# A graph network layer on one core: a new table of places that orders every step on its engine

## The chip, the cores and the metric

The kernel runs on one core of a Trainium2 chip. The core's engines work side by side: TensorE (PE in the profile, its weight loads PEld), VectorE (DVE), ScalarE (ACT), GpSimd (POOL) and the queue that issues most DMA transfers (SP). Each engine takes its instructions in the order in which the program gives them, and instructions of different engines wait for each other by semaphores. The metric is device time in microseconds (us); the median of three runs is given.

## The reference

A message passing layer on 128 graphs of 64 nodes with 128 features each. `x` is 128×64×128, `adj` is 128×64×64, zeros and ones; a node has itself as a neighbour, and some one in eight of the pairs is an edge.

```python
def _layernorm(x, g, b):
    mu = mean(x, -1); var = mean(square(x - mu), -1)
    return (x - mu) * rsqrt(var + 1e-5) * g + b
def _mlp(x, w0, b0, g0, be0, w1, b1, g1, be1, w2, b2):
    h = _layernorm(relu(x @ w0 + b0), g0, be0)
    h = _layernorm(relu(h @ w1 + b1), g1, be1)
    return h @ w2 + b2
pair_feats = concatenate([f_i, f_j], -1)          # every pair (i, j) of nodes of a graph
messages = _mlp(pair_feats, msg_...) * coupling_matrix[..., None]     # adj
agg = sum(messages, axis=2)
updated = part_feats + _mlp(concatenate([part_feats, agg], -1), upd_...)
```

All in float32.

## The kernel before

Only the edges are worked on. Two graphs make a pair p (64 of them); each graph gets 640 slots for its edges, and the slots of all graphs are cut into 160 chunks n of 512 edges. Five chunks make a quad q (32 of them), four pairs and ten chunks a block b (16 of them).

For a pair, `distance` (ACT, d), `make_tp` (DVE, tp) and `node_rows` (POOL) turn the adjacency into numbers of the first node of each edge slot; `marks` (PE, into the bank mk) and `compare` (DVE, j) find the second node; `stack` (DMA) puts both into one array s, which holds a one for each node of each edge. For a block, `turn_x` transposes x, and `rows` multiplies it by the two halves of the first weight (PE, into mu), from which `rows_hi` (ACT, abh) and `rows_lo` (DVE, abl) make a coarse and a fine part.

For a chunk: `gather` multiplies abl and abh by s (PE, into hps), `relu0` (ACT, h), `turn_h` (PE transposes into hT), `stats0` (DVE, two instructions st). The first layer norm is folded in: `root_of` (ACT, m20_sd) gives a standard deviation per edge, with which the bias of the second layer is scaled, either by `seed` (ACT, four instructions into the bank z0 or z1, for half of the chunks) or by `seed_all` (POOL, u). `layer1` (PE) then multiplies h by the weight w1c into that bank, `relu1` (ACT, or DVE with u) makes y, `stats1` (DVE) its statistics. For a quad, `var1_step` (POOL), `root1_of` (ACT), `inverse_of` (DVE) and `weights` (POOL, w) give each edge's factor, and `reduce` (PE, ys) sums y by node, once per block. A block's update follows in steps on four pairs: `sums_out` (ACT, ysum), `turn` (PE, ma) and `turn_out` (ACT, ysumT, uhT, uyT), the three layers (PE), their outputs and statistics (DVE), and the DMA of the result.

Every accumulator of PE (hps, hT, mk, ys, ma, mu, z0, z1) has one bank, so a step that fills a bank again waits for the engine that empties it.

The start has steps of its own (`marks_here`, `compare_here`, `rows_here` for the first two pairs) and matmuls without use that keep PE going (`keep_busy`, into ys).

No step is issued where it stands in the code. Each is entered into a plan with a nominal chunk n and a tag, and a table WHEN adds a number to its place:

```python
def at(n, tag, fn, *args):
    v = args[0] if args else 0
    v = v.b if isinstance(v, Unit) else v
    t = WHEN.get(f"{fn.__name__}{tag}", {}).get(n % 10 if 14 <= n < 138 else 100 + v, 0)
    plan.append((SCALE * n + t, len(plan), fn, args))
...
for _, _, fn, args in sorted(plan, key=lambda v: v[:2]):
    fn(*args)
```

SCALE is 144, so one chunk is 144 units. For n from 14 to 137 the table has one entry for each n modulo 10, so the order repeats every block; before and after, each step has an entry of its own (key 100 + its index). The sorted plan is the order of emission, and so the order on every engine. A second path for graphs with more edges than fit stands behind a condition and is not run with these inputs.

Of the kernel before, what the change touches and what calls it, by code (L numbers as in the profile page):

```python
# [9 lines left out]
F32 = mybir.dt.float32  # L10
# [42 lines left out]
    "count_out.0": {100: 79},
    "degrees": {9: -369, 101: -144, 102: -4, 115: -419},
    "degrees.0": {100: 58},
    "distance": {0: -532, 3: 185, 5: -470, 8: -359, 103: 34, 104: 302, 105: -163, 106: 312,
        107: -610, 108: 189, 158: -893, 159: -639, 160: -591, 161: -589, 162: 13, 163: -1137},
    "distance.0": {100: 163},
    "distance.1": {101: 208},
    "distance.2": {102: 283},  # L60
    "empties.0": {100: 156},
    "empties.1": {100: 154},
    "empties.10": {100: -158},
    "empties.11": {100: 84},
# [1592 lines left out]
```

## Time and profile before

| | |
|---|---|
| median of 3 runs (lowest to highest) | 496.4 us (495.78 to 496.48) |
| span of the profiled execution | 495.0 us |
| what lies around the span, by the median | 1.4 us |
| PE busy | 484.8 us (98%), 5947 instructions |
| DVE busy | 462.3 us (93%), 1225 |
| ACT busy | 397.9 us (80%), 907 |
| POOL busy | 353.0 us (71%), 563 |
| mean granted clock of TensorE | 0.995 |

The profiled execution has no time of its own beside its span, so the median of the runs stands for it. The span runs from the first to the last instruction. A row of the page's groups gives the line, engine, operation, output and inputs, the number of instructions, their busy time and mean length in ns, then the idle time of that engine just before them and what ended most of it. A row of the timeline gives the start, the length, the engine, the line, the operation, how many like it are joined, and in brackets the idle time before and its releaser. Matmuls overlap in a pipeline, so their rows are longer than the time from one to the next.

### The profile page before, as it was taken

Reading aid. Unit: us, or ns where it says so; the run is one execution under the profiler, and the core shown is the slowest. Engines: PE = TensorE matmul, PEld = TensorE weight load, DVE = VectorE, ACT = ScalarE, POOL = GpSimd, SP = SyncE. Lnnn points to the kernel's source line nnn. Section 1 sums busy time; section 2 is a strip of 40 time slices with the busy share of each in tenths; the row PEclk is TensorE's granted clock in tenths of the full one; section 3 lists DMA queues with packets and bytes.
Section 4 is the critical chain, followed back from the end, with each engine's and each line's share of the span. In section 5 each row is a group of like instructions: output and inputs, shape, how many; then the busy total and the mean of one; then the engine's idle time right before and its main releaser. Section 6 shows DMA issues by size and latency. Waiting matters only on the chain.

```text
span 495.0 us, 15915 instructions
## 1 busy us (share of the span) xinstructions
PE 484.8 (98%) x5947; PEld 461.3 (93%) x5947; DVE 462.3 (93%) x1225; ACT 397.9 (80%) x907; POOL 353.0 (71%) x563
## 2 busy tenths in 40 slices
PE   7999999999999999999999999999999999999994
PEld 5798999999999999999999999999999999999994
DVE  7989989999999999999999999999999999989975
ACT  7999978888787887878878787887878778767753
POOL 3276768878778787777779777787877678576661
PEclk9999999999999999999999999999999999999998
DMA  4676685667656575765757657466956775564311
GB/s 123 140 176 150 135 142 120 129 139 152 143 121 140 117 155 130 154 137 114 147 109 164 130 134 158 110 139 130 170 126 115 161 102 132 134 102 107 61 39 47
DMA packets 91474, 63.55 MB, mean 128 GB/s; under 512 B 57473, under 2 KB 75522, under 8 KB 91394
## 3 DMA queue, kind: packets, MB, share of 16 engines
q1 hardware_dynamic: 91106, 62.36, 60.4%
q8 instruction: 49, 0.80, 0.7%
q14 instruction: 31, 0.25, 0.1%
q10 hardware_dynamic: 288, 0.13, 0.1%
HBM read 7.15 MB, written 4.19 MB: 23 GB/s over the span
## 4 chain that ended last, share of the span: by engine, by line


## 5 line engine op out<-in xcount | busy, mean ns | idle before, releaser
L984 PE MATMUL z<-w1c,h 128*128 128x128 f32 x1280 | 190.0, 275 | 0.0
L984 PEld LDWEIGHTS z<-w1c,h 128*128 128x128 f32 x1280 | 171.7, 191 | 3.9 <-issue 0.4
L936 ACT ACTIVATE h<-hps,b0c 128x512 f32<-128x512 f32 x160 | 109.0, 681 | 42.3 <-PE hps L931 40.7
L627 DVE BATCH_NORM_STATS2 st<-hT 128x6 f32<-128x256 f32 x320 | 122.2, 418 | 15.3 <-PE hT L941 12.7
L627 DVE BATCH_NORM_STATS2 st<-y 128x6 f32<-128x256 f32 x320 | 125.3, 419 | 0.0
L978 ACT ACTIVATE z<-b1b,m_sd 128x128 f32<-128x128 f32 x320 | 118.4, 371 | 6.5
L941 PE MATMUL hT<-ident,h 128*128 128x128 f32 x640 | 113.3, 276 | 0.2 <-DVE st L627 0.2
L931 PE MATMUL hps<-s,abl 128*128 128x512 f32 (+3 forms) x256 | 97.0, 381 | 0.6 <-DVE abl L865 0.3
L971 POOL TENSOR_TENSOR u<-b1b,m_sd 128x512 f32<-128x512 f32 x80 | 87.5, 1103 | 7.8 <-ACT m_sd L635 7.7
L931 PE MATMUL hps<-s,abh 128*128 128x512 f32 (+3 forms) x256 | 92.2, 365 | 0.0
L941 PEld LDWEIGHTS hT<-ident,h 128*128 128x128 f32 x640 | 77.2, 141 | 2.9 <-PE z L984 0.6
L1027 POOL TENSOR_TENSOR w<-oh,m_q 128x192 f32<-128x192 f16 x126 | 65.2, 533 | 17.2 <-DVE m_q L656 9.6
L914 DVE TENSOR_TENSOR j<-mk,cmpt 128x320 fp32r<-128x320 f32 x124 | 59.3, 478 | 2.8 <-PE mk L906 1.2
L995 ACT ACTIVATE y<-z 128x512 f32<-128x512 f32 x80 | 47.9, 598 | 17.3 <-PE z L984 17.0
L611 DVE CUSTOM_DVE_ANT_0 y<-z,u 128x512 f32<-128x512 f32 x80 | 54.2, 678 | 1.7 <-PE z L984 0.2
L931 PEld LDWEIGHTS hps<-s,abl 128*128 128x128 f32 x256 | 48.8, 191 | 5.2 <-ACT ab L851 2.0
L889 POOL CAST i<-tp 128x640 fp32r<-128x640 f16 x58 | 41.8, 721 | 16.6 <-DMA s<-i 11.5
L874 ACT ACTIVATE d<-slot,mid 128x640 f16<-128x640 f16 x64 | 52.4, 822 | 0.4 <-DVE tp L880 0.3
L931 PEld LDWEIGHTS hps<-s,abh 128*128 128x128 f32 x256 | 49.5, 193 | 0.2
L645 POOL TENSOR_TENSOR m_v<-m_v,st 128x20 f32<-128x20 f32 x31 | 7.2, 232 | 57.5 <-DVE st L627 54.6
L1042 PE MATMUL ys<-y,w 128*32 128x128 f32 x1488 | 44.1, 274 | 0.0
L1042 PEld LDWEIGHTS ys<-y,w 128*32 128x32 f32 x1488 | 39.6, 110 | 2.6 <-issue 1.7
(193 smaller groups left out, 883.2 us busy)
## 6 DMA issues: line engine op xcount, KB each, us to landing
s<-j SPq DMA_DIRECT2D x124, 160.0 KB, 2.8
...
oh<-tp SPq DMA_TRANSPOSE x64, 3.5
...
```

Source lines behind the costliest of these rows:

```text
L611: nc.vector._custom_dve(TENSOR_ADD_SAT, out=o, in0=ps, in1=sb, s0=BIG, s1=0.0)
L627: nc.vector.bn_stats(st, src.rearrange("p t c -> p c t"))
L874: nc.scalar.activation(D[p], slot, AF.Abs, bias=blocks[b]["mid"][:, q:q + 1], scale=-1.0)
L914: nc.vector.tensor_tensor(JR[p][:, c], MK.pop((p, k))[:, 0:HC], cmpt[:, c], op=ALU.is_equal)
L931: nc.tensor.matmul(HP[n][:, c:c + w], lhsT=blocks[g // (2 * PB)]["ab", g // 4 % 2][k][:, g % 4, :], rhs=S[g // 2][:, g % 2, e:e + w], star ...
L936: nc.scalar.activation(H[n], HP.pop(n), AF.Relu, bias=b0c)
L941: nc.tensor.transpose(HT[n][:, t, :], H[n][:, t * P:(t + 1) * P], ident)
L971: nc.gpsimd.tensor_tensor(U[n], bc(W["b1b"], CH), SR[q][:, k:k + CH].unsqueeze(2).to_broadcast([P, CH, C]), op=ALU.mult)
L978: nc.scalar.activation(z_of(n)[:, t, :], W["b1b"], AF.Copy, scale=SR[q][:, k:k + 1])
L984: nc.tensor.matmul(ps[:, t, :], lhsT=H[n][:, t * P:(t + 1) * P], rhs=W["w1c"], start=by_vector(n) and t == 0, stop=True, skip_group_check= ...
L1027: (nc.vector if p == NP - 2 else nc.gpsimd).tensor_tensor(WT[p][:, g], oh, qs, op=ALU.mult)
L1042: nc.tensor.matmul(YS[b][g * N + m * HN:g * N + (m + 1) * HN, k, :], lhsT=w[:, g, m, u, :], rhs=y, start=(u == 0), stop=(u == TH - 1), til ...
```

## The change

The table WHEN is replaced as a whole: every number in it is new, for the start, for the ten chunks that repeat, and for the end. The operations, their sizes and their engines are the same. So that a step's two halves may come in either order, the code no longer lets the second half drop what the first one made: an entry is kept, or made by whichever half comes first. Line numbers behind the table move on by 44 to 49.

```diff
 WHEN = {
-    "bias0": {3: -1230, 112: -1975, 113: -1986, 114: 89},
+    "bias0": {3: -273, 112: -1205, 113: 4627, 114: -250},
...
-            nc.gpsimd.tensor_tensor(pos, blk.pop("rk"),
+            nc.gpsimd.tensor_tensor(pos, blk["rk"],
...
-                ps = blk["x_ps"] = bank()
+                ps = blk["x_ps", q0] = bank()
...
-            if k0 == 0:
+            if ("ab", half) not in blk:
...
-            if t:
-                del HT[n]
...
-            if t0:
-                del H[n]
...
-            if q == 0:
-                u.st = updp.tile([P, PB // 2, 6], F32, name=o + "_st", bufs=2)[:, 0:u.n // 2, :]
+            if o not in u.sts:
+                u.sts[o] = updp.tile([P, PB // 2, 6], F32, name=o + "_st", bufs=2)[:, 0:u.n // 2, :]
+            u.st = u.sts[o]
...
-            if q0 == 0:
-                u.usdb = wide("usdb", u)
+            u.usdb = wide("usdb", u)
...
+        def stacked(p):
+            if p not in S:
+                S[p] = sp.tile([P, 2, CAP], F32R, name="s")
+            return S[p]
...
-            nc.scalar.copy(S[p][0:N, g, :], TP[p][g * N:(g + 1) * N])
+            nc.scalar.copy(stacked(p)[0:N, g, :], TP[p][g * N:(g + 1) * N])
```

The order that follows from the table is shown at three places: here, and with the prediction's terms on the start and on 405 to 416 us. Here, PE's first steps before (keep-busy matmuls ys<-first, the count ma<-rk, the transposes of x):

```order
L1334 MATMUL ys<-first,mean_m 128x256 x3
L738 LDWEIGHTS lt
L738 MATMUL ma<-rk,lt 128x4
L817 MATMUL hT<-ident,xn 128x128 x2
L1334 MATMUL ys<-first,mean_m 128x256 x3
```

and now:

```order
L1378 MATMUL ys<-first,mean_m 128x256
L866 MATMUL hT<-ident,xn 128x128 x2
L787 LDWEIGHTS lt
L787 MATMUL ma<-rk,lt 128x4
L1378 MATMUL ys<-first,mean_m 128x256
```

Keep-busy matmuls (ys<-first) leave the front, and the transposes of x come ahead of the count.

More of the change, by code (lines that the diff above doesn't have):

```diff
@@ L53 @@
[L53 to L64, printed above, removed]
@@ L362 @@
[L362 to L369 removed]
+    "ahead.0": {100: 1294},
@@ new lines @@
+    "ahead.1": {100: 1381},
+    "ahead.10": {100: 1207},
+    "ahead.11": {100: 1227},
+    "ahead.2": {100: 1383},
+    "ahead.5": {100: 1177},
+    "ahead.8": {100: 1174},
+    "ahead.9": {100: 1292},
+    "bias0": {3: -273, 112: -1205, 113: 4627, 114: -250},
+    "bias0_0": {115: 5003},
+    "bias0_2": {115: 5107},
+    "bounds": {100: -14594},
+    "compare.0": {
+        0: 587, 2: 837, 5: 797, 7: 747, 102: 1118, 103: 1178, 104: 1168, 105: 1125, 106: 862,
+        107: 949, 158: 1530, 159: 2409, 160: 2710, 161: 3068, 162: 3099, 163: 3563},
@@ new lines @@
+    "compare.1": {
+        1: 634, 3: 773, 6: 789, 8: 788, 102: 1160, 103: 1346, 104: 1180, 105: 1073, 106: 909,
+        107: 901, 157: 1589, 158: 2373, 159: 2677, 160: 2770, 161: 3034, 162: 3341, 163: 3990},
+    "compare_here.0.0": {100: -65},
+    "compare_here.0.1": {100: 489},
+    "compare_here.1.0": {101: 915},
+    "compare_here.1.1": {101: 806},
+    "count": {8: 434, 101: 511, 102: 864, 115: 503},
+    "count.0": {100: -3294},
+    "count_out": {9: 456, 101: 544, 102: 897, 115: 671},
@@ new lines @@
+    "count_out.0": {100: -1998},
+    "degrees": {9: 588, 101: -401, 102: 662, 115: -74},
+    "degrees.0": {100: -2543},
+    "distance": {
+        0: -152, 3: 664, 5: 179, 8: 50, 103: -108, 104: 790, 105: 1117, 106: 1060, 107: 484,
+        108: 621, 158: 729, 159: 2363, 160: 1544, 161: 974, 162: 1864, 163: 2488},
+    "distance.0": {100: -1006},
+    "distance.1": {101: -794},
+    "distance.2": {102: 42},
+    "empties.0": {100: 1257},
+    "empties.1": {100: 1384},
+    "empties.10": {100: 1153},
@@ new lines @@
+    "empties.11": {100: 1207},
+    "empties.2": {100: 1150},
+    "empties.3": {100: 1041},
+    "empties.4": {100: 1028},
+    "empties.5": {100: 1083},
+    "empties.6": {100: 847},
+    "empties.7": {100: 755},
+    "empties.8": {100: 1049},
+    "empties.9": {100: 1299},
+    "finish": {8: 911, 110: 2286, 111: 3717, 112: 5020, 113: 4630, 114: 7758},
+    "finish_0": {115: 8726},
+    "finish_2": {115: 8952},
+    "flag_in": {100: 2993},
+    "flag_max": {100: 3882},
+    "flag_out": {100: 4972},
@@ new lines @@
+    "flag_sum": {100: 5071},
+    "flag_turn": {100: 3954},
[32 rows of a table added]
+    "inverse_of": {
[47 rows of a table added]
+    "layer_out.uh": {7: 736, 112: 3092, 113: 4332, 114: 4678},
+    "layer_out.uy": {2: 698, 111: 2886, 112: 3927, 113: 4905, 114: 5353},
[12 rows of a table added]
+    "load_adj": {1: -585, 102: -663, 103: -1980},
+    "load_x": {8: 125, 102: 924, 115: 1864},
+    "make_tp": {
+        1: 601, 4: 615, 6: 152, 9: 405, 103: 789, 104: 1179, 105: 1148, 106: 960, 107: 583, 158:
+        708, 159: 2442, 160: 1582, 161: 2628, 162: 2725, 163: 2620},
@@ new lines @@
+    "make_tp.0": {100: -674},
+    "make_tp.1": {101: 10},
+    "make_tp.2": {102: 761},
+    "marks.0": {
+        0: 579, 2: 662, 5: 792, 7: 653, 102: 1012, 103: 1123, 104: 1112, 105: 1083, 106: 820,
+        107: 809, 158: 1445, 159: 2316, 160: 2562, 161: 2862, 162: 2813, 163: 3538},
+    "marks.1": {
+        1: 568, 3: 741, 6: 770, 8: 734, 102: 1115, 103: 1301, 104: 1137, 105: 990, 106: 741,
+        107: 809, 157: 731, 158: 1421, 159: 2496, 160: 2656, 161: 2936, 162: 3056, 163: 3897},
+    "marks_here.0": {100: -148},
@@ new lines @@
+    "marks_here.1": {101: 691},
+    "node_marks": {
+        0: -440, 4: 504, 5: 1340, 9: 1826, 100: 1696, 101: 1292, 152: 3335, 153: -13, 154: 471,
+        155: 2024, 156: 3719, 157: 3402, 158: 4579, 159: 5392, 160: 5322, 161: 4942, 162: 4628,
+        163: 4875},
+    "node_rows": {
+        0: 835, 2: 511, 5: 519, 7: 715, 102: 1156, 103: 1566, 104: 1360, 105: 1046, 106: 961,
+        107: 761, 158: 1799, 159: 2322, 160: 1493, 161: 2955, 162: 2831, 163: 2546},
+    "odd_weights": {3: 522, 101: -504, 102: 114, 115: 2173},
@@ new lines @@
+    "odd_weights.0": {100: -3316},
+    "ones": {100: 9599},
+    "place": {1: 485, 101: 666, 102: 725, 115: 1376},
+    "place_first": {100: -1535},
+    "place_out": {3: 1019, 101: 795, 102: 663, 115: 2031},
+    "place_pair.0": {100: -694},
+    "place_rest": {100: -836},
+    "rank": {6: -49, 101: -626, 102: 1063},
+    "rank.0": {100: -4116},
+    "reduce.-1": {163: 4991},
+    "reduce.-2": {162: 4969},
+    "reduce.-3": {161: 4775},
+    "reduce.-4": {160: 4761},
+    "reduce.-5": {159: 4230},
@@ new lines @@
+    "reduce.-6": {158: 4167},
+    "reduce.-7": {157: 5153},
+    "reduce.-8": {156: 5141},
+    "reduce_block": {2: 777, 112: 1968, 113: 3143},
[17 rows of a table added]
+    "residual": {9: -528, 111: 4223, 112: 4605, 113: 5660, 114: 6537},
+    "residual_0": {115: 1852},
+    "residual_2": {115: -831},
+    "root1_of": {
+        0: 722, 5: 1018, 125: 1464, 126: 2445, 127: 2871, 128: 4011, 129: 4693, 130: 4501, 131:
+        4762},
+    "root_of": {
+        1: 596, 6: 669, 100: 1390, 101: 759, 127: 2289, 128: 2914, 129: 3045, 130: 3808, 131:
+        4902},
@@ new lines @@
+    "rows.0": {101: 903},
+    "rows.0.0.0.2": {100: -323},
+    "rows.0.0.2.4": {100: 1027},
+    "rows.1": {100: 829, 101: 666},
+    "rows_both": {8: -81, 114: -77, 115: 2678},
[28 rows of a table added]
+    "seed_all": {
[45 rows of a table added]
+    "sums_out": {4: 533, 112: 1904, 113: 3481, 114: 4277},
[46 rows of a table added]
+    "turn_out.uh": {1: 434, 111: 2327, 112: 3292, 113: 4767, 114: 4922},
+    "turn_out.uy": {6: 591, 111: 2633, 112: 4708, 113: 5054, 114: 5804},
+    "turn_out.ysum": {5: 499, 112: 2522, 113: 3487, 114: 4455},
+    "turn_out_0.uh": {115: 5584},
@@ new lines @@
+    "turn_out_0.uy": {115: 7399},
+    "turn_out_0.ysum": {115: 4892},
+    "turn_out_2.uh": {115: 5838},
+    "turn_out_2.uy": {115: 7318},
+    "turn_out_2.ysum": {115: 5473},
+    "turn_x": {6: -80, 101: 976, 115: 2749},
+    "turn_x.0": {100: -1310},
+    "turn_x.0.0.2": {100: -4860},
+    "turn_x_out": {7: -102, 101: 834, 115: 2757},
+    "turn_x_out.0.0.2": {100: -1388},
+    "turn_x_out_rest": {100: -199},
+    "upd_inverse": {4: 1414, 111: 4034, 112: 5401, 113: 5007, 114: 6528},
+    "upd_inverse_0": {115: 8265},
@@ new lines @@
+    "upd_inverse_2": {115: 8074},
+    "upd_m1": {2: 1589, 111: 3530, 112: 5663, 113: 5109, 114: 5938},
+    "upd_m1_0": {115: 6738},
+    "upd_m1_2": {115: 7379},
+    "upd_root0": {9: 803, 111: 1095, 112: 3390, 113: 4622, 114: 4879},
+    "upd_root0_0": {115: 5579},
+    "upd_root0_2": {115: 6311},
+    "upd_root1": {4: 1347, 111: 3313, 112: 5389, 113: 4945, 114: 6104},
+    "upd_root1_0": {115: 6764},
+    "upd_root1_2": {115: 7770},
+    "upd_shift": {9: 1017, 111: 1919, 112: 3823},
+    "upd_shift.0": {113: 5171, 114: 5070},
@@ new lines @@
+    "upd_shift.2": {113: 4896, 114: 4942},
+    "upd_shift_0.0": {115: 5873},
+    "upd_shift_2.0": {115: 6312},
+    "var1_step": {
+        3: 1276, 8: 976, 100: 810, 125: 1553, 126: 2583, 127: 3092, 128: 3831, 129: 4906, 130:
+        4767, 131: 4882},
+    "weights.0.0": {
+        0: 819, 5: 1203, 150: 1887, 152: 3043, 154: 3057, 156: 4963, 158: 4783, 160: 4811, 162:
+        4808},
+    "weights.0.1": {
+        1: 660, 6: 1087, 150: 1708, 152: 2652, 154: 3186, 156: 4547, 158: 4694, 160: 4598, 162:
+        4907},
@@ L370 @@
+    "weights.1.0": {
+        1: 755, 6: 1083, 151: 1454, 153: 3664, 155: 3004, 157: 5300, 159: 4842, 161: 4841, 163:
+        4891},
+    "weights.1.1": {
+        2: 770, 7: 1108, 151: 1336, 153: 3504, 155: 2917, 157: 5143, 159: 5050, 161: 4684, 163:
+        4852},
 }
@@ L796, in place_rest @@
             pos = adp.tile([P, PB, N], F32, name="pos")
-            nc.gpsimd.tensor_tensor(pos[:, 1:], blk.pop("rk")[:, 1:],
-                                    blk.pop("before")[:, 1:].unsqueeze(2)
+            nc.gpsimd.tensor_tensor(pos[:, 1:], blk["rk"][:, 1:],
+                                    blk["before"][:, 1:].unsqueeze(2)
                                     .to_broadcast([P, PB - 1, N]), op=ALU.add)
@@ L822, in turn_x_out @@
                 blk["xnT"] = blkp.tile([P, PB * P], F32, name="xnT", bufs=4)
-            nc.scalar.copy(blk["xnT"][:, q0 * P:q1 * P], blk.pop("x_ps")[:, q0 * P:q1 * P])
+            nc.scalar.copy(blk["xnT"][:, q0 * P:q1 * P], blk.pop(("x_ps", q0))[:, q0 * P:q1 * P])
         def rows(b, half, k0=0, k1=4):
@@ L1350, in compare_here @@
                 c = slice(k * HC, (k + 1) * HC)
[L1351 removed]
+                nc.vector.tensor_tensor(stacked(p)[N:P, g, c], MK[p, k][s, 0:HC], cmpt[s, c],
                                         op=ALU.is_equal)
[L1353 to L1354 removed]
         def ones():
@@ L1362, in turn_x_out_rest @@
         def turn_x_out_rest():
-            nc.scalar.copy(blocks[0]["xnT"][:, 2 * P:PB * P], blocks[0].pop("x_ps")[:, 2 * P:])
+            nc.scalar.copy(blocks[0]["xnT"][:, 2 * P:PB * P], blocks[0].pop(("x_ps", 2))[:, 2 * P:])
         early(".0", rank, 0)
```

123 lines of the change are left out of this document (1 added, 122 removed), and 438 rows, old and new, of the table WHEN.

## The prediction

> **What bounds the kernel now.** First the page's busy times and waits, then the windows by stage, then the timeline at the start and at 405 to 413 us. The chain of what ended last has no lines in this profile, so the path is argued from the windows and the waits. The page:
>
> ```profile
> span 495.0 us, 15915 instructions
> ...
> PE 484.8 (98%) x5947; PEld 461.3 (93%) x5947; DVE 462.3 (93%) x1225; ACT 397.9 (80%) x907; POOL 353.0 (71%) x563
> ...
> L936 ACT ACTIVATE h<-hps,b0c 128x512 f32<-128x512 f32 x160 | 109.0, 681 | 42.3 <-PE hps L931 40.7
> L627 DVE BATCH_NORM_STATS2 st<-hT 128x6 f32<-128x256 f32 x320 | 122.2, 418 | 15.3 <-PE hT L941 12.7
> ...
> L978 ACT ACTIVATE z<-b1b,m_sd 128x128 f32<-128x128 f32 x320 | 118.4, 371 | 6.5
> L941 PE MATMUL hT<-ident,h 128*128 128x128 f32 x640 | 113.3, 276 | 0.2 <-DVE st L627 0.2
> ...
> L995 ACT ACTIVATE y<-z 128x512 f32<-128x512 f32 x80 | 47.9, 598 | 17.3 <-PE z L984 17.0
> ```
>
> PE is busy 484.8 of 495.0 us. In the idle column (us of the engine before the group, then what ended it) ACT waits for PE 40.7 and 17.0 us, while PE waits 0.2 us for DVE before its 640 transposes. So PE sets the time, and ACT follows it. The sum below is made against the span of 495.0; the median of the runs, 496.4, lies 1.4 above it, and I carry that 1.4 over.
>
> The windows (window, its length, then busy us and instructions of PE, PEld, DVE, ACT, POOL, the granted clock, the DMA share, GB/s):
>
> ```profile
> 0.00:10.00 10.00, 7.31 (x39) 5.34 (x39) 7.02 (x21) 6.39 (x13) 4.27 (x15) 1.00 0.50 126
> 10.00:20.00 10.00, 9.28 (x96) 6.74 (x96) 9.55 (x26) 9.74 (x22) 2.67 (x6) 1.00 0.47 106
> 20.00:40.00 20.00, 19.78 (x216) 18.09 (x219) 18.18 (x48) 19.11 (x45) 11.95 (x16) 1.00 0.74 166
> 40.00:60.00 20.00, 19.72 (x205) 18.31 (x198) 19.23 (x53) 19.29 (x48) 13.47 (x25) 1.00 0.69 147
> 60.00:120.00 60.00, 60.00 (x748) 57.65 (x746) 57.40 (x146) 49.06 (x110) 47.48 (x72) 1.00 0.68 138
> ...
> 470.00:480.00 10.00, 10.00 (x188) 9.10 (x190) 9.09 (x27) 4.74 (x13) 5.70 (x12) 1.00 0.20 49
> 480.00:485.00 5.00, 5.00 (x62) 4.80 (x50) 2.96 (x8) 4.16 (x13) 3.25 (x5) 1.00 0.00 0
> 485.00:490.00 5.00, 3.71 (x27) 2.83 (x25) 4.46 (x18) 2.72 (x10) 0.58 (x3) 1.00 0.18 55
> ```
>
> Three stages. From 60 us to 485 PE is busy all the time and ACT four fifths: no order of the same instructions is shorter there, it can only add a wait. From 10 to 60 us PE idles 0.72 + 0.22 + 0.28 = 1.22 us and ACT only 0.26 + 0.89 + 0.71 = 1.86 of 50: there ACT is the bound beside PE. The start idles 2.69 us of PE, the end 1.29. All that can be won is in these.
>
> **The start (term one).** PE's rows before, from its second group of keep-busy matmuls (ys<-first, two records each) over the marks of pair 0 (mk, z) and the node products (mu) to the third group; three keep-busy matmuls, the count and two transposes stand ahead of them:
>
> ```order
> L1334 MATMUL ys<-first,mean_m 128x256 x3
> L906 LDWEIGHTS posall
> L906 MATMUL mk<-tp,posall 128x320
> L906 LDWEIGHTS posall
> L906 MATMUL z_250<-tp,posall 128x320
> L832 MATMUL mu<-w0a,xnT 32x128 x2
> L832 MATMUL mu<-w0b,xnT 32x128 x2
> L832 MATMUL mu<-w0a,xnT 32x128 x2
> L832 MATMUL mu<-w0b,xnT 32x128 x2
> L1334 MATMUL ys<-first,mean_m 128x256 x3
> ```
>
> Now, with one keep-busy matmul, two transposes and the count ahead (line numbers move on by 44 to 49):
>
> ```order
> L1378 MATMUL ys<-first,mean_m 128x256
> L866 MATMUL ma<-ident,xn 128x128 x2
> L881 MATMUL mu<-w0a,xnT 32x128 x2
> L881 MATMUL mu<-w0b,xnT 32x128 x2
> L881 MATMUL mu<-w0a,xnT 32x128 x2
> L881 MATMUL mu<-w0b,xnT 32x128 x2
> L1378 MATMUL ys<-first,mean_m 128x256
> L953 LDWEIGHTS posall
> L953 MATMUL mk<-tp,posall 128x320
> L953 LDWEIGHTS posall
> L953 MATMUL z_260<-tp,posall 128x320
> L1378 MATMUL ys<-first,mean_m 128x256 x5
> ```
>
> The node products moved ahead of the marks, keep-busy work from the front to behind them. On DVE, from the first tp to the first abl, before:
>
> ```order
> L880 TENSOR_SCALAR tp<-d,deg 128x640
> L729 SCALAR_TENSOR_TENSOR rk<-first,an 128x256
> L880 TENSOR_SCALAR tp<-d,deg 128x640
> L1351 TENSOR_TENSOR s<-mk,cmpt 64x320
> L1351 TENSOR_TENSOR s<-z_250,cmpt 64x320
> L1351 TENSOR_TENSOR s<-mk,cmpt 64x320
> L1351 TENSOR_TENSOR s<-z_250,cmpt 64x320
> L865 TENSOR_TENSOR abl<-mu,abh 128x256
> ```
>
> and now:
>
> ```order
> L929 TENSOR_SCALAR tp<-d,deg 128x640
> L778 SCALAR_TENSOR_TENSOR rk<-first,an 128x256
> L1400 TENSOR_TENSOR s<-mk,cmpt 64x320
> L1400 TENSOR_TENSOR s<-z_260,cmpt 64x320
> L929 TENSOR_SCALAR tp<-d,deg 128x640
> L914 TENSOR_TENSOR abl<-mu,abh 128x256
> L1400 TENSOR_TENSOR s<-mk,cmpt 64x320
> L1400 TENSOR_TENSOR s<-z_260,cmpt 64x320
> ```
>
> abl moved ahead of the second pair of compares. The timeline (start, us, engine, line):
>
> ```profile
> 1.91 2.93 PE L1334 MATMUL ys<-first,mean_m 128*128 128x256 f32 x6 [1.91 <-DVE first L519]
> ...
> 4.62 0.21 PE L738 MATMUL ma<-rk,lt 128*128 128x4 f16 x1
> ...
> 5.16 1.76 PE L1334 MATMUL ys<-first,mean_m 128*128 128x256 f32 x6
> ...
> 6.94 0.71 DVE L880 TENSOR_SCALAR tp<-d,deg 128x640 f16<-128x640 f16 x1
> ...
> 7.68 0.83 ACT L874 ACTIVATE d<-slot,mid 128x640 f16<-128x640 f16 x1 [0.27 <-DVE tp L880]
> ...
> 7.70 0.30 PE L906 MATMUL mk<-tp,posall 128*128 128x320 f16 x1 [0.79 <-DVE tp L880]
> ...
> 8.50 0.72 ACT L1345 CAST s<-tp 64x640 fp32r<-64x640 f16 x1
> 8.56 0.48 DVE L1351 TENSOR_TENSOR s<-mk,cmpt 64x320 fp32r<-64x320 f32 x1
> ...
> 8.64 1.56 PE L1334 MATMUL ys<-first,mean_m 128*128 128x256 f32 x6
> ...
> 9.13 0.36 ACT L854 CAST abh<-mu 128x256 fp32r<-128x256 f32 x1
> ...
> 10.39 0.42 DVE L865 TENSOR_TENSOR abl<-mu,abh 128x256 fp32r<-128x256 f32 x1
> ...
> 10.87 0.50 PE L931 MATMUL hps<-s,abl 128*128 128x512 f32 x1 [0.34 <-DVE abl L865]
> ...
> 11.64 0.69 ACT L936 ACTIVATE h<-hps,b0c 128x512 f32<-128x512 f32 x1
> ```
>
> The chain to the marks (7.70, released by tp) keeps its steps. Behind it abl at 10.39 held the gather. Two compares fewer (0.48 each) stand ahead of abl now, and ACT casts s and abh straight behind tp: abl starts near 9.4. The third compare, which frees the bank of mk for the next marks, then ends near 10.2. Ten keep-busy records (a row of six takes 1.56; less the drain, for which I take the 0.21 of the 4-column ma row, 0.225 each) hold PE from 8.0 to 10.25; then two marks (0.30 together): gather at 10.6, 0.27 earlier. On ACT: s 0.72, abh 0.36, a small cast some 0.2, d 0.83, a copy like abh, d 0.83, s 0.72 are 4.0 from 7.68, less overlaps of up to 0.1 each: 11.1 to 11.7. First h at 11.4 instead of 11.64: −0.25 (ends −0.5 and 0).
>
> **The ramp to 60 us (term two).** I counted ACT's rows ahead of each h in both orders, priced by their rows. Ahead of the 19th, 20th and 22nd h they are the same to 0.1 us; ahead of the 9th to 18th there is up to 1.3 us more now (d, the casts and seeds come sooner). No ACT work leaves the ramp, so only ACT's idle 1.86 us can shrink: gain between 0 and 1.86. More work ready ahead shortens waits of ACT for hps, but as the content is level at the 19th, I take a fifth, −0.4. The compares come 1 to 2 us of work earlier, with them SP's transfers of j; a transfer gains lead, which costs nothing. If that cover went, PE's gather would wait for part of the landing.
>
> **60 to 405 us (term three).** Ten-chunk pattern repeated. PE has no idle time, so at best 0. DVE's stats of y now sit between the two stats of hT more often, and PE's next transposes need those; PE's 0.2 us wait there in 495 says the cover is ample. Cost 0; if the cover went, one st (0.42) for each of some 13 repeats.
>
> **405 to 416 us (term four).** Here the repeat ends (n = 138) and steps get places of their own. ACT before; h is relu0, y relu1, z the seeds that layer1 adds onto:
>
> ```order
> L936 ACTIVATE h_7880<-hps_7871,b0c_75 128x512
> L978 ACTIVATE z0_7898<-b1b_449,m20_sd_7686 128x128
> L635 ACTIVATE um0_sd_7905<-uh_st_7752,eps_c_115 128x4
> L978 ACTIVATE z0_7898<-b1b_449,m20_sd_7686 128x128 x3
> L874 ACTIVATE d_7926<-slot_139,mid_7852 128x640
> L936 ACTIVATE h_7978<-hps_7911,b0c_75 128x512
> L635 ACTIVATE m20_sd_7982<-st0_7722,eps_c_115 128x20
> L978 ACTIVATE z1_7984<-b1b_449,m20_sd_7982 128x128 x4
> ```
>
> and now:
>
> ```order
> L1038 ACTIVATE y_7920<-z0_7829 128x512
> L1023 ACTIVATE z0_7936<-b1b_456,m20_sd_7696 128x128 x3
> L983 ACTIVATE h_8000<-hps_7897,b0c_75 128x512
> L923 ACTIVATE d_8009<-slot_139,mid_7323 128x640
> L1023 ACTIVATE z0_7936<-b1b_456,m20_sd_7696 128x128
> L684 ACTIVATE m20_sd_8017<-st0_7682,eps_c_115 128x20
> L1023 ACTIVATE z1_8019<-b1b_456,m20_sd_8017 128x128 x3
> L1141 COPY uhT_8025<-ma_7837 128x512
> L1023 ACTIVATE z1_8019<-b1b_456,m20_sd_8017 128x128
> L1117 COPY ysum_8028<-ys_7946 128x512
> L983 ACTIVATE h_8038<-hps_8002,b0c_75 128x512
> ```
>
> A y now heads the group. It waits for PE's z0_7829, and behind it in ACT's order stand all four seeds of z1_8019; layer1's first matmul on z1_8019 waits once, for the last of the four. The rows of before at this place:
>
> ```profile
> 407.40 1.17 ACT L978 ACTIVATE z<-b1b,m_sd 128x128 f32<-128x128 f32 x3
> 408.51 0.81 ACT L874 ACTIVATE d<-slot,mid 128x640 f16<-128x640 f16 x1
> 409.23 0.67 ACT L936 ACTIVATE h<-hps,b0c 128x512 f32<-128x512 f32 x1
> 409.80 0.31 ACT L635 ACTIVATE m_sd<-st,eps_c 128x20 f32<-128x20 f32 x1
> 410.14 1.58 ACT L978 ACTIVATE z<-b1b,m_sd 128x128 f32<-128x128 f32 x4
> ...
> 413.13 0.58 ACT L1097 COPY uhT<-ma 128x512 f32<-128x512 f32 x1
> ...
> 407.50 0.43 PE L931 MATMUL hps<-s,abl 128*128 128x384 f32 x1
> ...
> 408.67 2.83 PE L1042 MATMUL ys<-y,w 128*32 128x128 f32 x96
> 411.43 0.39 PE L931 MATMUL hps<-s,abl 128*128 128x256 f32 x1
> ...
> 412.34 0.61 PE L984 MATMUL z<-w1c,h 128*128 128x128 f32 x4
> 412.79 0.27 PE L941 MATMUL hT<-ident,h 128*128 128x128 f32 x1
> ```
>
> Before, the last seed ended at 410.14 + 1.58 = 411.72 and PE came to it at 412.34: 0.6 to spare. Now, from the end of z0_7829, start to start: y after 0.2 (the drain), then y 0.50 (0.598 less an overlap of 0.1), three seeds 1.11, h 0.57, d 0.72, a seed 0.37, m_sd 0.34, three seeds 1.11, the uhT copy 0.55, the last seed 0.38: 5.85. PE meanwhile: from 411.43 to 412.34 four 256-wide gathers and three transposes take 0.91, so 0.13 a piece, 1.04 with the fourth transpose; the rest of the gather ahead of ys is 407.50 to 408.67, 1.17, less a 384-wide piece (0.2) and a mark, plus a transpose: 0.97; ys to its next row 2.76; z0_7936 is four instructions of two records, four records taking 0.45: 0.90. Sum 5.67. So PE waits about 0.2, and the ysum copy ahead of h_8038 (0.55, against 0.90 of z1 on PE beside 0.55 + 0.57 on ACT) keeps the next gather another 0.2: +0.4. Ends: 0, as both sums are good to 0.4, and 0.9 with every overlap of y, h, d and seeds gone (y 0.598, h 0.681).
>
> **The end (term five).** From 440 us three more places have y ahead of the seeds, with spare of about nothing: +0.1 (0 to 0.9). POOL's last w come behind an m0; POOL is busy 5.70 of 10 us there, so cost 0, else a part of one such step, under 1. The last layers stay a chain with the same steps: 0 ± 0.2.
>
> **Sum.** −0.25 − 0.4 + 0 + 0.4 + 0.1 = −0.15: span 494.85, time 496.25, say 496.3. What a measurement of this kernel tells from no change is about 0.2%, 1.0 us.
>
> **Rivals.** (a) Faster: ACT hardly idles in the ramp. Its full 1.86 is won instead of 0.4, the other terms hold: 496.3 − 1.45 = 494.9. For it: ACT's rows read 97%, and PE idles 1.22 there only because ACT is late. Against: ACT's content is level at the 19th h. It decides if ACT idles under about 0.9 us from 10 to 60 us.
>
> (b) Slower: the matmul clock starts later. The first six keep-busy records took 2.93 us, the next 1.76 and 1.56: by the sixth of each, one record of the second row was still slow, so PE ran slow until some 5.6 us, though the granted clock reads 1.00. With six records ahead of the marks instead of twelve, the ten behind the marks may start slow, each up to (2.93 − 1.56) / 6 = 0.23 longer: 2.3 if all, about 1 if half, and they stand ahead of the gather. With 1.2 the time is 497.5. It decides if those ten take over 3 us. [...]
>
> (c) Slower: the passages cost their upper end, 0.9 and 0.9 in place of 0.4 and 0.1: 496.3 + 1.3 = 497.6. For it: one wait covers four seeds. Against: before had 0.6 to spare. It decides if ACT's seeds end over 0.5 us behind PE there.
>
> **How the numbers follow.** My sum 0.42; (a) 0.24; (b) 0.15; (c) 0.15; 0.04 for what I do not see. The sum's own range is 495.2 to 497.3, and of its 0.42 about 0.09 lies over 1 us below 496.4 and 0.05 above. Faster: 0.23 of (a) and 0.09, with 0.02: 0.34. Slower: 0.12 of (b), 0.12 of (c), 0.05, 0.02: 0.31. Same: 0.35. The range runs from (a) with a better start, 494.4, to (b) near all slow, 498.4.
>
> **What the profile after would show.** Gather at about 10.6 and first h at 11.4; ten keep-busy records in some 2.3 us; ACT idle of 1.4 in 10 to 60; PE still 60.00 of 60 in the middle; an idle of PE before z<-w1c near 411 to 416, released by ACT's z. The prediction fails if PE waits for DVE's st in the repeated part, or if the ramp's waits move by more than 1 us.

## The result and the profile after

The new table makes the kernel slower: 511.8 us (median of 4 runs, 511.02 to 512.37) against 496.1 in the same measurement (495.58 to 496.48), a ratio of 1.0312 with a 95% interval of 1.0297 to 1.0327. That is 15.7 us, and outside the range of 494.4 to 498.4. The profiled execution took 511.38 us with a span of 509.5, 14.5 above the span before; the rest of the 15.7 is the spread of executions and what lies around the span.

The page after, its first lines and two groups (columns as before):

```profile
span 509.5 us, 15878 instructions
...
PE 497.1 (98%) x5947; PEld 461.3 (91%) x5947; DVE 464.1 (91%) x1225; ACT 398.0 (78%) x907; POOL 352.9 (69%) x563
...
L988 PE MATMUL hT<-ident,h 128*128 128x128 f32 x640 | 126.5, 276 | 0.6 <-DVE st L676 0.5
...
L1085 PEld LDWEIGHTS ys<-y,w 128*32 128x32 f32 x1488 | 40.2, 110 | 8.6 <-POOL w L1070 5.7
```

PE still reads 98%, with the same 5947 instructions: 12.3 us more "busy" for the same work. A matmul's row is longer here than the time to the next start (the reduce's records are 0.27 us long and start some 0.03 us apart, before and after), so a short wait leaves no idle time between the rows, and PE's share hides the loss. The weight loads show it: their busy time is 461.3 in both and its share of the span falls from 93% to 91%, where PE's reads 98% in both. In the second group the idle time ahead of the reduce's weight loads is put down to POOL's w, 5.7 us. The same group before has no wait for w:

```profile
L1042 PEld LDWEIGHTS ys<-y,w 128*32 128x32 f32 x1488 | 39.6, 110 | 2.6 <-issue 1.7
```

The windows by stage, after (window, length, then busy us and instructions of PE, PEld, DVE, ACT, POOL, clock, DMA share, GB/s):

```profile
10.00:60.00 50.00, 49.33 (x505) 43.05 (x505) 46.75 (x123) 47.19 (x109) 26.91 (x43) 1.00 0.63 146
60.00:405.00 345.00, 342.61 (x4264) 321.55 (x4263) 320.69 (x835) 272.86 (x613) 258.18 (x400) 1.00 0.65 131
```

and the same two windows before:

```profile
10.00:60.00 50.00, 48.78 (x507) 43.15 (x507) 46.96 (x125) 48.15 (x112) 28.10 (x46) 1.00 0.67 146
60.00:405.00 345.00, 345.00 (x4367) 333.58 (x4366) 331.44 (x865) 281.31 (x634) 266.18 (x415) 1.00 0.66 137
```

In the same 345 us of the repeated part PE gets through 4264 matmuls instead of 4367. Most of the loss sits there, and every engine does less.

To place it, the table has the start of each block's reduce (the ys rows of PE), and the time from the first to the last start of the 160 small matmuls of the reduce and the rows that follow it (start to start, since the ends are modelled):

| | first reduce | twelfth reduce | between | one steady block | the 160 matmuls in it |
|---|---|---|---|---|---|
| before | 62.52 | 384.09 | 321.57 | 29.33 | 4.30 |
| after | 63.39 | 396.99 | 333.60 | 30.39 | 4.99 |

So 0.87 us is lost ahead of the first reduce, 12.03 in the eleven blocks between, and 1.61 behind the twelfth (509.51 − 396.99 against 495.00 − 384.09). In nine of the twelve reduces of after the 160 matmuls take 0.69 us longer: 6.2 us.

What they wait for is seen on POOL. One block after, POOL's timeline from the first layer norm's variance (m_v) to the last factors w of the block:

```profile
209.04 0.23 POOL L694 TENSOR_TENSOR m_v<-m_v,st 128x20 f32<-128x20 f32 x1 [1.84 <-DVE st L676]
209.23 1.28 POOL L1129 TENSOR_TENSOR xo<-xn,cu2b 128x512 f32<-128x512 f32 x1
210.76 0.72 POOL L938 CAST i<-tp 128x640 fp32r<-128x640 f16 x1 [0.25 <-DVE tp L929]
211.44 1.40 POOL L1070 TENSOR_TENSOR w<-oh,m_q 128x192 f32<-128x192 f16 x2
212.79 0.98 POOL L938 CAST i<-tp 128x640 fp32r<-128x640 f16 x1
213.73 1.03 POOL L1183 TENSOR_TENSOR usdb<-bu1b,um_sd 128x512 f32<-128x512 f32 x1
214.73 1.03 POOL L1016 TENSOR_TENSOR u<-b1b,m_sd 128x512 f32<-128x512 f32 x1
215.73 1.05 POOL L1070 TENSOR_TENSOR w<-oh,m_q 128x192 f32<-128x192 f16 x2
```

and the same block before:

```profile
199.02 0.23 POOL L645 TENSOR_TENSOR m_v<-m_v,st 128x20 f32<-128x20 f32 x1 [2.09 <-DVE st L627]
199.22 0.72 POOL L889 CAST i<-tp 128x640 fp32r<-128x640 f16 x1
200.55 1.05 POOL L1027 TENSOR_TENSOR w<-oh,m_q 128x192 f32<-128x192 f16 x2 [0.61 <-DVE m_q L656]
...
203.52 1.04 POOL L1139 TENSOR_TENSOR usdb<-bu1b,um_sd 128x512 f32<-128x512 f32 x1 [0.47 <-ACT um_sd L635]
204.52 0.51 POOL L1027 TENSOR_TENSOR w<-oh,m_q 128x192 f32<-128x192 f16 x1
204.99 2.04 POOL L971 TENSOR_TENSOR u<-b1b,m_sd 128x512 f32<-128x512 f32 x2
206.98 0.69 POOL L1027 TENSOR_TENSOR w<-oh,m_q 128x192 f32<-128x192 f16 x1
```

PE's reduce of that block, after:

```profile
214.17 3.40 PE L1085 MATMUL ys<-y,w 128*32 128x128 f32 x94
```

and before:

```profile
208.08 2.17 PE L1042 MATMUL ys<-y,w 128*32 128x128 f32 x72
```

Before, the last w ended at 207.67, ahead of the reduce itself. After, the reduce starts at 214.17 and the last two w run from 215.73 to 216.78. POOL does not take longer: from the start of m_v to the end of the last w it was 8.65 us and is 7.74. But PE's reduce now comes 5.13 us behind m_v instead of 9.06. The last w has lost 3.93 − 0.91 = 3.02 us of lead.

### The profile page after: what moved, and what is told of

It reads as the page before. It is cut to its first block, busy times and chain, and to the rows that moved or that the text cites. A ratio compares the mean times of both kernels' runs of the same rounds, so it can differ in the third digit from the quotient of the medians.

```text
span 509.5 us, 15878 instructions
## 1 busy us (share of the span) xinstructions
PE 497.1 (98%) x5947; PEld 461.3 (91%) x5947; DVE 464.1 (91%) x1225; ACT 398.0 (78%) x907; POOL 352.9 (69%) x563
## 5 line engine op out<-in xcount | busy, mean ns | idle before, releaser
L1029 PE MATMUL z<-w1c,h 128*128 128x128 f32 x1280 | 177.6, 278 | 0.4 <-ACT z L1023 0.2
L1029 PEld LDWEIGHTS z<-w1c,h 128*128 128x128 f32 x1280 | 160.3, 192 | 3.4 <-ACT z L1023 1.5
L676 DVE BATCH_NORM_STATS2 st<-hT 128x6 f32<-128x256 f32 x320 | 126.3, 417 | 10.6 <-PE hT L988 8.9
L988 PE MATMUL hT<-ident,h 128*128 128x128 f32 x640 | 126.5, 276 | 0.6 <-DVE st L676 0.5
L978 PE MATMUL hps<-s,abl 128*128 128x512 f32 (+3 forms) x256 | 99.7, 390 | 0.8 <-issue 0.7
L1016 POOL TENSOR_TENSOR u<-b1b,m_sd 128x512 f32<-128x512 f32 x80 | 83.4, 1044 | 15.8 <-ACT m_sd L684 15.7
L988 PEld LDWEIGHTS hT<-ident,h 128*128 128x128 f32 x640 | 79.6, 141 | 12.3 <-PE z L1029 2.9
L1070 POOL TENSOR_TENSOR w<-oh,m_q 128x192 f32<-128x192 f16 x126 | 66.8, 551 | 27.7 <-DVE m_q L705 17.6
L938 POOL CAST i<-tp 128x640 fp32r<-128x640 f16 x58 | 44.7, 770 | 51.0 <-DVE tp L929 47.6
L1085 PE MATMUL ys<-y,w 128*32 128x128 f32 x1488 | 49.2, 275 | 1.3
L953 PE MATMUL mk<-tp,posall 128*128 128x320 f16 x126 | 38.4, 304 | 0.2
```

The costliest lines, as they stand in the source:

```text
L676: nc.vector.bn_stats(st, src.rearrange("p t c -> p c t"))
L978: nc.tensor.matmul(HP[n][:, c:c + w], lhsT=blocks[g // (2 * PB)]["ab", g // 4 % 2][k][:, g % 4, :], rhs=S[g // 2][:, g % 2, e:e + w], star ...
L988: nc.tensor.transpose(HT[n][:, t, :], H[n][:, t * P:(t + 1) * P], ident)
L1016: nc.gpsimd.tensor_tensor(U[n], bc(W["b1b"], CH), SR[q][:, k:k + CH].unsqueeze(2).to_broadcast([P, CH, C]), op=ALU.mult)
L1029: nc.tensor.matmul(ps[:, t, :], lhsT=H[n][:, t * P:(t + 1) * P], rhs=W["w1c"], start=by_vector(n) and t == 0, stop=True, skip_group_check= ...
L1070: (nc.vector if p == NP - 2 else nc.gpsimd).tensor_tensor(WT[p][:, g], oh, qs, op=ALU.mult)
```

## The experiments

All ratios are against the kernel before, run on the same chip in the same measurement (its medians lie from 495.99 to 496.28). Where an edit moves steps, the diff shows the rows of that engine's order.

**e1 and e2: which part of the table.** In e1 only the ten repeated chunks have new places, in e2 only the start and the end. The kernels hold the resulting order as a list; here it is written as the choice of the table:

```diff
-    t = WHEN[...]
+    t = (NEW if 14 <= n < 138 else OLD)[...]     # e1; e2 has NEW and OLD changed over
```

> The new order only for the steps with nominal chunk 14 to 137 (the part that repeats), the old order for the start and the end. The traces put 12.0 of the 15.7 us lost between the first and the twelfth reduce. Both theories (late weights on POOL; many small waits in a loop of ACT, DVE and PE) expect 507 to 509 us. If the start or the seam at chunk 138 were what loses, it would stay under 500.

> The opposite: the new order for the start and the end only, the old one for the part that repeats. Expected 497 to 499 us: 0.9 us lost before the first reduce and 1.6 after the twelfth, less if the end was late only because the repeated part left it so. My prediction's terms on the start, the ramp, 405 to 416 us and the end, without term three, would have it at 496.2.

Measured: e1 517.5 us, 1.0429 (1.0410 to 1.0449); e2 513.6 us, 1.0355 (1.0338 to 1.0372). Both are far above what was expected. Neither total prices its part, because the seams between two orders cost more than the parts: behind the twelfth reduce e1 loses 7.5 us and e2 7.7 (after loses 1.6), and ahead of the first e1 loses 1.9 and e2 5.9 (after 0.9). Far from a seam the blocks tell: a steady block takes 30.39 us in e1, as in after, and 29.33 in e2, as in before. The loss per block belongs to the repeated places.

**e3 and e4: POOL's places alone.** In e3 POOL's steps have their old places (counted from relu0's) and all others new ones; a few steps differ from that near the end. In e4 the factors w of the repeated part come 36 to 365 units earlier (a quarter of a chunk to two and a half). Written again as the choice of the table:

```diff
+    # e3: a step of POOL keeps its old place
+    if engine(fn) is POOL: t = OLD[...]
+    # e4
+    if fn is weights and 14 <= n < 138: t -= ...     # 36 to 365, by step
```

> The new order on all engines, but POOL's own steps take their old places (scaled by the places of relu0). Late weights: the wait of ys for w, about 0.58 us per block in the new order, goes, and with it 6 us: 505 to 506.5. Small waits in a loop: something else ends last instead, 509 to 512.

> The new order, only the steps weights (POOL, w) of the repeated part are moved forward to where their factor m_q is there, ahead of the casts i, usdb and u. Late weights: 505 to 507, PE's wait for POOL's w gone. A loop: usdb and u come 1 us later, DVE waits for them, and PE for DVE, 509 to 513.

Measured: e3 556.9 us, 1.1229 (1.1210 to 1.1248); e4 533.7 us, 1.0751 (1.0726 to 1.0776). Both are much worse than after, and than any of the expectations. POOL's waits in e3 (line, what for, total us, times, longest):

```profile
POOL m_v L558 <- DVE st L540: 79.6, 13, 7.1
POOL w L931 <- DVE m_q L569: 46.4, 25, 6.6
```

and in e4:

```profile
POOL w L931 <- DVE m_q L569: 37.2, 27, 3.2
```

A w placed ahead of its own factor (m_q, from DVE) doesn't come sooner; it holds up everything behind it on POOL. In after that wait is 17.6 us in 12. Both runs show that the places of one engine can't be chosen apart from the others', and neither tells what w's lateness costs in after.

**e5: the last two w ahead of usdb and u,** eleven times, POOL's rows:

```diff
 w x2
 i
+w x2
 usdb
 u
-w x2
 u
```

> The new order with one edit on POOL, 11 times: the last two w of a block go ahead of usdb and u (they stood behind them; their factor m_q is there by then). Late weights: the two waits of ys for w (0.55 us a block) go, 11 times: 505 to 507. If usdb, 1 us later, is waited for in its place (DVE's uy already waits 0.8 us for it): 510 to 515.

Measured: 521.4 us, 1.0508 (1.0488 to 1.0529), above both expectations. The reduce's wait is gone, its 160 matmuls take 4.30 us again, but a block takes 31.36. PE's waits:

```profile
PE hT L849 <- DVE st L540: 9.5, 11, 1.1
PE mk L814 <- DVE j L822: 5.1, 11, 0.5
```

and DVE's:

```profile
DVE uy L524 <- POOL usdb L1044: 17.4, 11, 1.8
```

usdb is now the late one: DVE waits for it before uy (7.3 us in after), and DVE's st and j behind uy come late for PE, 0.9 and 0.5 us in each of eleven blocks. That is the wait by which the prediction said it would fail (PE for DVE's st); it is real, but after has it once, for 0.5 us. POOL has too little room there for both w and usdb.

**e6 and e7: less work on POOL, or on DVE.** In e6 xo is cut to 4 columns; in e7 DVE's test for weights other than 0 and 1 is left out.

```diff
-            nc.gpsimd.tensor_tensor(u.xo, u.blk["xn"][:, u.q, :], bc(W["cu2b"], u.n),
+            nc.gpsimd.tensor_tensor(u.xo[:, :, 0:4], u.blk["xn"][:, u.q, 0:4],     # e6
...
-            nc.vector.scalar_tensor_tensor(a2, an, 1.0, an, op0=ALU.subtract, op1=ALU.mult)
-            nc.vector.tensor_reduce(nball[:, b:b + 1], ...)                        # e7
```

> The new order, with POOL's xo (1.28 us a block, in the queue between m_v and w) cut to four columns, its first column used for all, so the output leaves out most of that term. Nothing is reordered. Late weights by a full POOL queue: w comes 1 us earlier, the waits of ys go: 504 to 506. If w is late because m_v comes late and POOL is not short of time: 510 to 512.

> The new order without the steps odd_weights (DVE, a and nball, 0.8 us a block; the test for weights other than 0 and 1 is left out). If DVE's queue makes the many small waits (some 0.5 us a block beside those for w): 506 to 510. Late weights alone: 511 to 512.

Measured: e6 507.8 us, 1.0235 (1.0218 to 1.0252); e7 508.9 us, 1.0259 (1.0242 to 1.0277). In e6 the 160 matmuls take 4.62 us and a block 30.02: both 0.37 less than in after. In e7 they take 4.73 and a block 30.12: 0.26 and 0.27 less. What w gains, the block gains, one for one. In the eleven blocks e6 wins 3.1 us and e7 2.9; nine times 0.37 are 3.3. Of xo's 1.28 us most is not won, because i then waits for DVE's tp instead (1.06). The time of e7 is the one expected if DVE's queue made the small waits, but the trace does not show that: its gain sits in the reduce, since w comes 0.26 us sooner there too.

**e8: the start's keep-busy matmuls where they were before,** PE's rows:

```diff
-ys<-first
+ys<-first x3
 hT<-ident,xn x2
 ma<-rk,lt
-ys<-first
 ma<-ident,xn x2
+ys<-first x3
 mu<-w0a,xnT ... (rows)
-ys<-first
 mk, z (marks)
-ys<-first x5
+ys<-first x2
```

> The new order with the keep-busy matmuls of the start where the old order has them (six records in front, six ahead of the marks, four behind them). The traces show the new order's first marks at 8.26 us, behind two keep-busy records that took 1.22. If the slow clock made that: first marks at 7.7, first gather at 10.7 instead of 11.30, and 0.3 to 0.6 us off the time: 511.3. If it does not matter: 511.8.

Measured: 511.3 us, 1.0315 (1.0294 to 1.0337): no difference to after that can be told. The start didn't get better: the first transposes and the count now stand behind six slow records (the count at 5.05 instead of 4.60), the first marks come at 8.87 instead of 8.26 and the gather at 11.76 instead of 11.30. The time is the one expected if the slow matmuls made the loss, but by luck: the marks and the gather came later, not sooner, and starts of 128x256 matmuls stay 0.43 us apart until 7.4 us in this run too. So it doesn't test what it should, the slow matmuls alone.

**e9 and e10: make w late in the kernel before.** The old order, with the last w of each repeated block behind posall (1.6 us later), or behind posall, i and two m as well (4.6 us later), POOL's rows:

```diff
 w
 u x2
-w
 posall x2
+w          # e9
 i
 m x2
+w          # e10, in place of e9's
```

> The old order with one edit on POOL alone, 12 times: the last w of a block goes behind posall (1.6 us) instead of ahead of it. In the trace of before the last w ends at 207.67, ys starts at 208.08 and comes to that w some 2 us later, so 0.8 us stay to spare. Late weights as a matter of a threshold: no change, 496 us. If any w that comes later is paid for: up to 1.6 us a block, 510 or more.

> The same edit with a larger dose: the last w of 11 blocks goes behind posall, i and both m0 (4.6 us together), so it ends near 212.2 where ys wants it near 210.1. Late weights: 2.1 us a block, 11 times, 519 us, with PE's wait shown before ys, released by POOL's w. If the old order is so loose that the wait is made up later in the block: under 510.

Measured: e9 497.3 us, 1.0020 (1.0009 to 1.0030); e10 527.7 us, 1.0634 (1.0608 to 1.0660). PE's wait in e10:

```profile
PE ys L946 <- POOL w L931: 23.2, 11, 3.1
```

In e10 the 160 matmuls take 6.61 us in the steady blocks, 2.31 more, and a block takes 31.62, 2.29 more. So of 4.6 us the first 2.3 are free and the rest is paid in full in every block; e9's 1.6 lies under that, and its steady blocks are those of before (29.31). Most of what e9 loses shows at the twelfth reduce, whose 160 matmuls take 5.63 us instead of 4.30. This is w's lead in the kernel before: 2.3 us. After has lost 3.02 of it, and 2.3 − 3.02 = −0.7: the 0.69 us that its reduces are longer. The total of e10, 31.5 us, is above 11 × 2.3 = 25; its first, fourth and eleventh reduces are longer still.

**e11 and e12: is it ACT, or all three?** e11 cuts ACT's copies of uhT, uyT and ysumT to 128 columns; e12 has the edits of e6, e7 and e11.

```diff
-            nc.scalar.copy(getattr(u, src + "T"), u.ps[:, 0:u.n * P])
+            nc.scalar.copy(getattr(u, src + "T")[:, 0:P], u.ps[:, 0:P])
```

> The new order with ACT's three copies uhT, uyT and ysumT of a block cut to their first 128 columns, which then stand for all four pairs (the output is not the layer's): 1.2 us of ACT a block less, nothing reordered. The small waits of the new order (0.4 us a block over the old order's, behind uhT, the seeds and h) are ACT's: 3 to 5 us off, 507 to 509. If they are DVE's or POOL's: 511 to 512.

> All three reliefs at once in the new order: POOL's xo cut to four columns, DVE's a and nball left out, ACT's three copies cut (so the output is not the layer's). If the new order loses because all three engines are late by some tenths where PE needs them: 500 to 503, close to the old order. If what is relieved only uncovers the next wait: 505 to 508.

Measured: e11 512.2 us, 1.0311 (1.0292 to 1.0331), as after: ACT is not it, and the short gaps of PE are the same to 0.01 us. e12 507.2 us, 1.0213 (1.0196 to 1.0230): the 160 matmuls take 4.44, so 0.14 of the reduce's 0.69 is left. In a steady block (29.83) the reliefs of e6 and e7 nearly add: 0.56 of 0.37 and 0.27. In the total they don't, and the expected 500 to 503 was missed; two single blocks (30.73 and 30.46) and a first reduce at 64.19 instead of 63.39 take part of it back. Some 0.5 us per steady block over before is left with all three engines lightened, 0.14 of it in the reduce.

**e13 and e16: the count and the weight load behind it.** In after the 4-column count stands ahead of four matmuls of layer1, in before ahead of a mark. e13 moves it ahead of a mark in the new order, e16 ahead of layer1 in the old one, twelve times each, PE's rows:

```diff
-ma<-rk,lt        # e13, new order
 z<-w1c,h
 ...
+ma<-rk,lt
 mk<-tp,posall
```

```diff
-ma<-rk,lt        # e16, old order
 mk<-tp,posall
+ma<-rk,lt
 z<-w1c,h
```

> The new order with one edit on PE, 12 times: the 4-column count (ma<-rk) goes from its place just ahead of a layer1 matmul (z<-w1c) to just ahead of a mark (mk). If the gap of 0.08 us that PE shows behind the count in every block is the weight load of z that a 0.03 us matmul can't cover, it goes: 0.08 x 12 = 1 us less, 510.8, and the gap is gone from the trace. If it is a wait for another engine it stays: 511.8.

> The mirror in the old order: the count, which stands ahead of a mark there, changes places with it, so it stands just ahead of a layer1 matmul, 12 times. If the short matmul ahead of a weight load is the cause: 0.05 to 0.08 us a block, 0.6 to 1 us, 496.8 to 497.2, with the gap in the trace. If not: 496.2.

Measured: e13 510.6 us, 1.0285 (1.0268 to 1.0302), 1.2 below after; e16 496.9 us, 1.0012 (1.0003 to 1.0022). After, PE's rows at one count:

```profile
228.45 0.17 PE L787 MATMUL ma<-rk,lt 128*128 128x4 f16 x1
228.48 0.69 PE L1029 MATMUL z<-w1c,h 128*128 128x128 f32 x4
```

and in e13, the same four of layer1, now without the count ahead:

```profile
228.27 0.61 PE L890 MATMUL z<-w1c,h 128*128 128x128 f32 x4
```

in e16:

```profile
226.96 0.17 PE L648 MATMUL ma<-rk,lt 128*128 128x4 f16 x1
226.99 0.69 PE L890 MATMUL z<-w1c,h 128*128 128x128 f32 x4
```

Behind the count four matmuls of layer1 take 0.69 us, otherwise 0.61: 0.08 in each block, which goes and comes with that one place. A steady block takes 30.31 in e13 against 30.39 in after, and 29.40 in e16 against 29.33 in before. The totals alone would not carry this: the intervals of e13 and after overlap.

**e14 and e15: give w its lead back on PE's side.** The half of the rows that goes into ma (0.9 us of small matmuls) stands ahead of the reduce instead of behind it, twelve times; POOL's order is untouched. e15 has e13's move too.

```diff
+ma<-w0a,xnT / ma<-w0b,xnT   (32 records)
 ys<-y,w
-ma<-w0a,xnT / ma<-w0b,xnT
 mu<-w0a,xnT / mu<-w0b,xnT
```

> The new order with one edit on PE, 12 times: half of rows (eight small matmuls into ma, 0.9 us), which stood behind ys, goes ahead of it, so that PE reaches the last two w 0.9 us later; POOL is left as it is. If w is late only against ys: the two waits (0.55 us a block) go and nothing takes their place, 505 to 506.5. If the block is held by the whole loop of POOL, DVE and PE: 509 to 512.

> Both edits, of count and of rows: 504 to 505.5 if each cause stands by itself; 508 or more if not. Still above the old order's 496, as the other short gaps, the start (0.7 us up to 60 us) and the end (1.6 us) stay.

Measured: e14 506.2 us, 1.0205 (1.0188 to 1.0222), 5.6 below after; e15 505.8 us, 1.0188 (1.0170 to 1.0206). The reduces' 160 matmuls, counted from the rows that now come first, are at 4.30 again in all steady blocks, and no wait for POOL's w is left among the weight loads; the longest sum of them is now

```profile
PEld hT L850 <- PE z L891: 3.6, 11, 0.3
```

A block takes 29.91 in e14 and 29.83 in e15: 0.48 and 0.56 less than after, not 0.69, since the mark behind the reduce now comes 0.17 us late. The eleven blocks of e14 are 4.7 us shorter than after's. This is the cleanest test of the cause: no work is taken away and no queue but PE's is touched. No version beat the kernel before.

## Why the prediction was wrong

**Term three failed (60 to 405 us, "cost 0"): it cost 12.0 us.** The step that failed is "PE has no idle time, so at best 0", followed by weighing a single wait, DVE's st before the transposes, and calling its cover ample. That wait only went from 0.2 to 0.5 us. The wait that came was another engine's, POOL's w before the reduce, whose lead was not looked at. Nor did "PE has no idle time" say that nothing waits: PE's rows overlap, and PE, forecast at 60.00 of 60, reads 342.61 of 345 where the eleven blocks lost 12 us. The trace of before had the lead: the last w ended at 207.67, and the reduce from 208.08 comes to it after 76 of its 96 records (there PE waits in after and in e10), 76 × 0.0274 = 2.1 us later, so the lead was some 2.5 us (e10 measured 2.3). Of the new order, xo, i, two w, i, usdb, u and two w behind m_v, at the mean durations of before, make some 7.0 us from m_v to the last w. PE's records between m_v and the reduce fall from 77 to 43, and the 5.13 us that the 43 take in after, with the 2.1, put the use of the last w 7.2 us behind m_v. So even by old durations the lead falls from 2.5 to about 0.2: a warning, not yet the loss. The trace of after has the rest: i waits 0.25 for tp, and one w and one i take 0.93 and 0.98 instead of 0.51 and 0.72. Why these two were longer was not tried.

What the 12.03 us consist of: nine reduces with 0.69 more, 6.2 (e14 takes the 0.69 out of all of them; e6, e7 and e10 show the one for one). The count, 11 × 0.08 = 0.9 (e13, e16). Of a block's 1.06 that leaves 0.3, 3.3 in all, in small gaps of each block; the clearest are 0.07 between two update matmuls (mu<-u1c) and 0.05 between two of layer1 at two places. PE's starts at these places were the same to 0.01 us when ACT had less to do (e11). That they come, like the count's, from which matmul stands ahead of which fits this but was not tried. The last 1.6 are longer waits in single blocks, mostly of gathers; they were not taken apart.

**Term one (the start, −0.25) had the wrong sign: +0.43 at the gather.** PE's rows after:

```profile
1.91 1.22 PE L1378 MATMUL ys<-first,mean_m 128*128 128x256 f32 x2 [1.91 <-DVE first L568]
4.14 0.66 PE L866 MATMUL hT<-ident,xn 128*128 128x128 f32 x2 [1.01 <-DMA xn<-in_x_dram]
...
7.24 1.22 PE L1378 MATMUL ys<-first,mean_m 128*128 128x256 f32 x2
8.26 0.47 PE L953 MATMUL mk<-tp,posall 128*128 128x320 f16 x1
...
8.73 2.32 PE L1378 MATMUL ys<-first,mean_m 128*128 128x256 f32 x10
...
11.30 0.50 PE L978 MATMUL hps<-s,abl 128*128 128x512 f32 x1
```

The two records at 7.24 took 1.22, the same as the first two at 1.91; the ten from 8.73 took 2.32, as forecast. By starts, 128x256 matmuls come 0.43 us apart at first and 0.22 apart later, though the granted clock reads 1.00 from 0 to 10 us before and after. I call the first the slow spacing; that a matmul clock makes it, as rival (b) took it, no run shows. It lasted until some 8.7 us instead of 5.6, so the marks, forecast to keep their 7.70, came at 8.26, though tp was there at 7.62 (7.65 before). Behind them the third compare ended at 10.99 instead of 10.2, the second marks waited for it, and the gather came at 11.30 instead of 10.6, the first h at 12.08 instead of 11.4.

e14 has this same start, and in its trace the slow spacing ended sooner:

```profile
7.33 0.70 PE L1240 MATMUL ys<-first,mean_m 128*128 128x256 f32 x2
7.87 0.30 PE L815 MATMUL mk<-tp,posall 128*128 128x320 f16 x1
...
10.82 0.51 PE L840 MATMUL hps<-s,abl 128*128 128x512 f32 x1
```

There the gather comes at 10.82, 0.48 sooner than in after and 0.05 sooner than before. In e5, with the same start again, the slow spacing lasted until 10.6, the ten records behind the marks took 3.17, and the gather came at 12.08. So slow matmuls that last longer, as rival (b) had them, are there, and by its own sign (ten records over 3 us) it came true in e5; in after the slow matmuls stood only ahead of the marks. How much it costs differs from run to run with the same order of PE's start: in the eleven runs that have it the gather comes between 10.82 and 12.08. That the sign came out so in after is in part luck. In the five with the old start the slow spacing ended between 4.6 and 6.9 us, and the gather came at 10.87 or 10.88 in all of them, because PE stood idle 0.26 to 1.15 us ahead of the first marks anyway. The new start lost that slack, which the prediction did not count, and even in e14, where that spacing ended sooner, its gain was 0.05 and not 0.27. PE's work up to 8.26 has a gap of 1.01 us ahead of the first transposes, and the 0.22 spacing came 3.1 us later than before (8.7 against 5.6). That the one made the other was not shown: no run here changes the gap alone.

**Term two (the ramp, −0.4) had the wrong sign.** ACT's idle time from 10 to 60 us was forecast at 1.4 and is 50 − 47.19 = 2.81 (1.85 before), so rival (a) is out. Of the 0.87 lost ahead of the first reduce, 0.43 is the start's and 0.44 the ramp's in these two traces. By which waits was not tried.

**Term four (the passage, +0.4) was right in place and mechanism, and in its total by luck.** It comes ten us later in the trace than forecast, as the loss ahead of it had moved it. ACT's rows:

```profile
421.22 0.60 ACT L1038 ACTIVATE y<-z 128x512 f32<-128x512 f32 x1 [0.69 <-PE z L1029]
...
426.01 0.58 ACT L1141 COPY uhT<-ma 128x512 f32<-128x512 f32 x1
426.49 0.37 ACT L1023 ACTIVATE z<-b1b,m_sd 128x128 f32<-128x128 f32 x1
```

and PE's:

```profile
426.06 0.61 PE L1029 MATMUL z<-w1c,h 128*128 128x128 f32 x4
426.91 1.16 PE L1029 MATMUL z<-w1c,h 128*128 128x128 f32 x8 [0.24 <-ACT z L1023]
```

From y's start to the end of the last seed is 426.86 − 421.22 = 5.64 (the working had 5.85 with the drain of 0.2). PE's four records from 426.06 last 0.45 start to start, so it waited 0.40, until the last of the four seeds was there. The working had 0.2 for this wait and 0.2 for the next gather, behind the ysum copy; PE's rows show no such second wait.

**Term five (the end, +0.1) was too small.** Behind the twelfth reduce 1.61 us are lost; less the passage's 0.4, 1.2 are left where the upper bound was 0.9. What of it is which of the three other places was not tried. Rival (c), the passages at 0.9 each, is so near its price, but not by its own sign (a wait over 0.5 us; it was 0.40), and 1.6 is a small part of 14.5.
